# Normalization coefficients of a scan kernel: part of their arithmetic moved to GpSimd and TensorE, with the stages of five groups set further apart

## The chip, the cores and the metric

One core of a Trainium2 chip runs one program. The engines are TensorE (PE, matmuls; its weight loads are shown as PEld), VectorE (DVE), ScalarE (ACT), GpSimd (POOL) and SyncE (SP, which here only issues DMAs). Each has a queue of its own that it works through in order, and semaphores tie them together. The metric is the device time of the program in microseconds (us), as the median of several executions; lower is better.

## The reference

Two layers of the same form work on x of shape (32, 48, 64, 128): batch, channels, rows, columns, in float32. A layer normalizes its input over groups of three channels, then runs four recurrences over it, and adds the result to its input:

```python
def _gn(v, G=16, eps=1e-5):
    g = v.reshape(B_, G, C_ // G, H_, W_)
    m = jnp.mean(g, axis=(2, 3, 4), keepdims=True)
    s = jnp.var(g, axis=(2, 3, 4), keepdims=True)
    return ((g - m) / jnp.sqrt(s + eps)).reshape(v.shape)
def step(w, b):
    def f(carry, inp):
        nxt = inp + _conv1d(carry, w, b)
        return (nxt, nxt)
    return f
...
x = x + _L0_conv_ref(_gn(x), ...)
x = x + _L1_conv_ref(_gn(x), ...)
```

Within a layer the recurrence goes down the rows, up again, then right along the columns, and left again. Each step is a convolution of five taps (48 to 48 channels) over the other image axis, applied to the state of the step before. So a layer has 63 + 63 steps over rows and 127 + 127 over columns that depend on each other.

What the change touches is `_gn`: the mean and the variance of each image and channel group have to become a scale and an offset for each channel (scale = 1/sqrt(var + eps), offset = −mean × scale).

## The kernel before, in words

**Tiling.** The 32 images are worked on in four groups of eight (GB = 8). Eight neighbouring positions times 48 channels fill three tiles of 128 partitions (NG = 3). A step (`step`, L693) is nine matmuls of 128x128 (L706), 128 columns wide, into three PSUM tiles; each PSUM tile is evicted by one DVE operation (L715) that adds the bias and the step's input and writes the new state. The next step's matmuls read it.

**Phases.** `PHASES` (L102) lists twelve phases: for each layer four row phases (one for each group of images, 126 steps) and two column phases (one for each pair of groups, 254 steps). Together they are 2,024 steps, run one after the other.

**The agenda.** All other work is put between the steps by hand. `at(t, fn, ...)` (L785) books a function for step t of the whole scan; `catch_up` (L1124) calls what is due ahead of each step, and `in_order` (L231) fixes the order of the instructions on each engine to the order of these calls. `spread(t, gen, 1)` (L788) calls a generator once at each step from t on: each `yield` in it pushes what follows one step later. So an instruction stands in its engine's queue behind all that was booked earlier, and if it waits, everything behind it in that queue waits too: on PE and DVE that is the scan.

**The coefficients.** `scaling` (L289) makes scale and offset of one group of eight images. It first takes the means and variances of parts from one of three classes: `InputStats` (for the input, groups x0 to x3), `ResultStatsV` (for layer 0's result, statistics by DVE) and `ResultStatsA` (the same, with sums taken by ACT); for the result the groups are r0 to r3. The classes' `__call__` merges the parts. Then `average` sums over the three channels of a group by matmuls with a mask (L298), `expand` brings the result back to all partitions by three matmuls (L302), and short DVE operations stand between: differences from the mean (L325), their squares (L326), the variances added (L327), and at the end a reciprocal (L348) of ACT's Sqrt (L344), one Newton step (L350 to L353), scale (L360) and offset (L361). A float32 matmul of these shows as two passes on PE in the trace. For the input there is one mask (n = 1), and `average` and `expand` of the mean are done with the same source; for the result there are three (n = 3), and the average is copied out of PSUM before it is expanded.

**When.** x0 is done ahead of the scan, in `first_group`. x1, x2 and x3 are booked in `plan_input` (L798, L816): x1 ends in phase 0, x2 runs in phase 2 (the first column phase) around step 410, x3 in phase 4. r0 and r1 run in phase 3 around steps 557 and 577, r2 and r3 in phase 7, twenty steps apart (L932, L933).

**What runs beside them.** GpSimd adds the residuals of a column phase (`add_residual`, L635, L638), six units of 128x2048 for each quarter of the columns; it also permutes pieces of the input (`permute`, L536, sixteen copies of 112x256 for each piece of four rows for both halves), fills weight tiles with zeros (L266) and keeps a row (booked at L841, shown as L236). ACT applies the coefficients (`scale_rows`, L579, 24 or 48 operations for a load) and takes statistics of the input (`take_others`, L395 and L403) and of the result (L470, L476). In phase 3 group 3 of the input is brought in through one buffer: each piece's permutes and statistics must be through before the next piece's load can write there.

Of the kernel before, what the change touches and what calls it, by code (L numbers as in the profile page):

```python
# [31 lines left out]
ALU = mybir.AluOpType  # L32
# [9 lines left out]
GB = 8  # L42
# [76 lines left out]
def kernel(  # L119
# [166 lines left out]
    def stat_tile(shape, name, key):  # L286
        return stat_pool.tile(shape, F32, tag=name, name=f"{name}_{key}")

    def scaling(key, layer, g, averages, masks):  # L289
# [3 lines left out]
        yield from averages(key)  # L293
        mean_p, var_p = averages.result

        def average(ps, rhs):
            for i in range(n):
                nc.tensor.matmul(ps, masks[i], rhs[:, i], start=i == 0, stop=i == n - 1)  # L298

        def expand(ps, rhs):  # L300
            for o in range(NG):
                nc.tensor.matmul(ps[:, o], maskp[:, o], rhs, start=True, stop=True)  # L302
# [9 lines left out]
        mean_c = stat_tile([P, GB], "mean_c", key)  # L312
        nc.vector.tensor_copy(mean_c, ps[0:P, 0])
        yield
        if n > 1:
            expand(ps[:, 1 : 1 + NG], mean_c)
            yield
        mean = small("mean")
        if n > 1:
            nc.vector.tensor_copy(mean, ps[:, 1 : 1 + NG])  # L320
        at = mean if n > 1 else mean_c.unsqueeze(1)
        np_ = FULL if n > 1 else P
        spare = small("dev")
        dev = spare[0:np_, 0:n]
        nc.vector.tensor_tensor(dev, mean_p, at, ALU.subtract)  # L325
        nc.vector.tensor_tensor(dev, dev, dev, ALU.mult)  # L326
        nc.vector.tensor_tensor(dev, dev, var_p, ALU.add)  # L327
        yield
        if n == 1:
            expand(ps[:, 2 + NG :], dev[:, 0])  # L330
            nc.vector.tensor_copy(mean, ps[:, 1 : 1 + NG])
        else:
            average(ps[0:P, 1 + NG], dev)
# [12 lines left out]
        yield  # L346
        r0 = std
        nc.vector.reciprocal(r0, std)  # L348
        t0 = spare
        nc.vector.tensor_tensor(t0, var, r0, ALU.mult)  # L350
        nc.vector.tensor_tensor(t0, t0, r0, ALU.mult)
        yield
        nc.vector.tensor_scalar(t0, t0, -0.5, 1.5, ALU.mult, ALU.add)  # L353
# [6 lines left out]
        nc.vector.tensor_tensor(scale, r0, t0, ALU.mult)  # L360
        nc.vector.scalar_tensor_tensor(offset, mean, -1.0, scale, ALU.mult, ALU.mult)  # L361
        coeffs[layer, g] = scale, offset

    class InputStats:
# [48 lines left out]
        def __call__(self, key):  # L413
            mv = self.mv
            yield
# [772 lines left out]
```

## Time and profile before

| | us |
|---|---|
| three runs, median (lowest to highest) | 4323.13 (4319.51 to 4324.4) |
| the profiled execution, its time | 4327.19 |
| its span in the trace | 4325.4 |
| PE busy in the span | 4072.9 |
| DVE busy | 2177.4 |
| ACT busy | 1337.2 |
| GpSimd busy | 891.9 |

The scan itself lasts from the end of step 0 at 113.6 us to the end of the last step at 4241.5 us; the last results then go out until the end of the span. The mean granted clock of PE was 0.979 of full speed. The 6,072 evictions by DVE last 348 ns each; they are the beat by which steps are counted in what follows, step 0 being the first of phase 0.

A word on reading: in the timeline a row gives the start, the length, the engine, the source line, the operation, what it writes and reads, the shape, how many instructions the row merges, and in brackets the engine's idle time ahead of the first one with what ended it. A view by groups has the busy time and the mean of one in place of start and length.

The groups of DVE operations that belong to the coefficients, each four times over the program unless noted (mean of one):

| line | for x (112x8 or 128x24) | for r (128x24) |
|---|---|---|
| L313 copy of the mean from PSUM | 158 ns | 155 ns |
| L325 difference | 1100 ns | 183 ns (two groups of two) |
| L326 square | 1323 ns | 184 ns |
| L327 variance added | 1322 ns | 182 ns (two groups of two) |
| L348 reciprocal | 296 ns | 295 ns |
| L350, L351 Newton step | 252, 355 ns | 183, 182 ns |
| L353 Newton step, L360 scale | 280, 365 ns | 168, 183 ns |
| L361 offset | 274 ns | 183 ns |

### The profile page before, as it was taken

Reading aid. Unit: us, or ns where it says so; the run is one execution under the profiler, and the core shown is the slowest. Engines: PE = TensorE matmul, PEld = TensorE weight load, DVE = VectorE, ACT = ScalarE, POOL = GpSimd, SP = SyncE. Lnnn points to the kernel's source line nnn. Section 1 sums busy time; section 2 is a strip of 40 time slices with the busy share of each in tenths; the row PEclk is TensorE's granted clock in tenths of the full one; section 3 lists DMA queues with packets and bytes.
Section 4 is the critical chain, followed back from the end, with each engine's and each line's share of the span. In section 5 each row is a group of like instructions: output and inputs, shape, how many; then the busy total and the mean of one; then the engine's idle time right before and its main releaser. Section 6 shows DMA issues by size and latency. Waiting matters only on the chain. (4 is left out here: it accounts for less than half of the span.)

```text
span 4325.4 us, 89999 instructions
## 1 busy us (share of the span) xinstructions
PE 4072.9 (94%) x36624; PEld 4042.5 (93%) x36624; DVE 2177.4 (50%) x6554; ACT 1337.2 (31%) x2656; POOL 891.9 (21%) x859
## 2 busy tenths in 40 slices
PE   3898998998999999998999999999999999999992
PEld 1898998998999999998999999999999999999992
DVE  6344444446764445444446655444444444444443
ACT  1683301344794554300005773513000002110122
POOL 3472001234323010000004310000000024510352
PEclk9999999999999999999999999999999999999996
DMA  9999799966998989769507989929289049999999
GB/s 165 183 188 166 111 157 158 235 130 191 237 204 138 158 152 159 117 115 174 131 1 218 220 173 144 153 45 160 47 136 202 1 77 242 249 241 158 176 197 183
DMA packets 2117983, 680.35 MB, mean 157 GB/s; under 512 B 2006688, under 2 KB 2057408, under 8 KB 2077632
## 3 DMA queue, kind: packets, MB, share of 16 engines
q1 hardware_dynamic: 2019552, 582.30, 71.9%
q10 hardware_dynamic: 94816, 86.00, 9.7%
q0 software_dynamic: 3200, 6.30, 0.6%
q8 instruction: 288, 4.72, 0.5%
q14 instruction: 127, 1.04, 0.1%
HBM read 397.57 MB, written 295.99 MB: 160 GB/s over the span
## 5 line engine op out<-in xcount | busy, mean ns | idle before, releaser
L579 ACT ACTIVATE arena<-arena,offset,scale 128x256 f32<-128x256 f32 (+2 forms) x816 | 576.4, 800 | 423.9 <-PE step_12u L706 120.5
L638 POOL TENSOR_TENSOR arena<-arena 128x2048 f32<-128x2048 f32 x80 | 362.8, 4548 | 1469.2 <-PE step_10l L706 459.0
L536 POOL COPY arena<-arena 112x256 f32<-112x256 f32 x458 | 271.2, 651 | 561.5 <-DMA arena<-in_x 282.6
L706 PE MATMUL step_00r<-arena,early 128*128 128x128 f32 x2286 | 252.4, 274 | 15.3 <-DMA arena<-upa 14.2
L706 PEld LDWEIGHTS step_00r<-arena,early 128*128 128x128 f32 x2286 | 251.9, 187 | 15.8 <-issue 15.8
L706 PE MATMUL step_01r<-arena,early 128*128 128x128 f32 x2286 | 251.6, 274 | 14.0 <-DMA arena<-upa 14.0
L706 PEld LDWEIGHTS step_01r<-arena,early 128*128 128x128 f32 x2286 | 251.4, 187 | 14.2 <-issue 14.1
L706 PE MATMUL step_11r<-arena,early 128*128 128x128 f32 x2286 | 252.1, 274 | 8.6 <-DVE arena L715 8.6
L706 PEld LDWEIGHTS step_11r<-arena,early 128*128 128x128 f32 x2286 | 251.6, 187 | 9.0 <-DVE arena L715 8.9
L470 ACT ACTIVATE early<-arena 128x256 f32<-128x256 f32 x192 | 129.6, 675 | 412.2 <-DMA arena<-xin 319.9
L706 PE MATMUL step_00l<-arena,wleft 128*128 128x128 f32 x2286 | 252.2, 274 | 0.0
L706 PEld LDWEIGHTS step_00l<-arena,wleft 128*128 128x128 f32 x2286 | 251.8, 187 | 0.0
L706 PE MATMUL step_10l<-arena,wleft 128*128 128x128 f32 x2286 | 249.1, 272 | 0.0
L706 PE MATMUL step_11l<-arena,wleft 128*128 128x128 f32 x2286 | 249.1, 272 | 0.0
L706 PE MATMUL step_01l<-arena,wleft 128*128 128x128 f32 x2286 | 249.1, 272 | 0.0
L706 PE MATMUL step_10r<-arena,early 128*128 128x128 f32 x2286 | 249.1, 272 | 0.0
L706 PEld LDWEIGHTS step_10l<-arena,wleft 128*128 128x128 f32 x2286 | 249.0, 186 | 0.0
L706 PEld LDWEIGHTS step_11l<-arena,wleft 128*128 128x128 f32 x2286 | 249.0, 186 | 0.0
L706 PEld LDWEIGHTS step_01l<-arena,wleft 128*128 128x128 f32 x2286 | 249.0, 186 | 0.0
L706 PEld LDWEIGHTS step_10r<-arena,early 128*128 128x128 f32 x2286 | 249.0, 186 | 0.0
L663 ACT COPY arena<-arena 128x256 f32<-128x256 f32 x172 | 99.6, 656 | 404.2 <-POOL arena L638 152.9
L403 ACT ACTIVATE early<-arena 112x512 f32<-112x512 f32 x192 | 121.1, 631 | 305.6 <-DMA arena<-in_x 237.7
(176 smaller groups left out, 7070.1 us busy)
## 6 DMA issues: line engine op xcount, KB each, us to landing
arena<-in_x SPq DMA_DIRECT2D x48, 768.0 KB, 12.7
xin<-arena SPq DMA_DIRECT2D x96, 384.0 KB, 5.6
arena<-xin SPq DMA_DIRECT2D x96, 384.0 KB, 8.9
mid<-arena SPq DMA_DIRECT2D x96, 384.0 KB, 7.9
arena<-mid SPq DMA_DIRECT2D x192, 192.0 KB, 4.3
upb<-arena SPq DMA_DIRECT2D x192, 192.0 KB, 3.9
arena<-upb SPq DMA_DIRECT2D x96, 384.0 KB, 12.7
arena<-xin SPq DMA_DIRECT2D x186, 192.0 KB, 4.2
```

Source lines behind the costliest of these rows:

```text
L403: nc.scalar.activation(junk[0:P], piece, AF.Identity, accum_out=self.sum[:, at[0], at[1]],)
L470: nc.scalar.activation(junk[:, 0:n], view[:, b], AF.Identity, accum_out=self.sum[:, i, j : j + 1])
L536: copy(dst[:, r, q], src[:, r0 + r, q])
L579: nc.scalar.activation(args[0], args[0], AF.Identity, bias=args[2], scale=args[1])
L638: eng.tensor_tensor(unit, unit, nat, ALU.add)
L663: copy(by_w(perm)[:, a], src[:, a])
L706: nc.tensor.matmul(part(whole(ps[o])[0:m], -s), weights[:, i, at : at + m], part(src(i), s), start=seen[o] == 1, stop=seen[o] == left[o],)
```

## The change

Four things are changed in `scaling` and in the classes ahead of it.

- The difference from the mean reads the mean in PSUM, where `expand` or `average` left it. With one mask the copy of the mean into SBUF goes, and with it one step of distance.
- The variances are no longer added to the squares by DVE: `average` (three masks) and `expand` (one mask) take two terms and add them in PSUM, so such a group of matmuls doubles.
- With `slack` above 0, the squares, the Newton step, scale and offset, and in the classes' `__call__` the differences, squares and sums of the parts, are issued on GpSimd instead of DVE. Operations that multiply and add in one (`scalar_tensor_tensor`) are split in two, on either engine. The reciprocal, the reductions and all that reads PSUM stay on DVE.
- With `slack`, that many more steps lie ahead of the matmuls that read the squares, ahead of the reciprocal, and (in the classes) ahead of the reduction of the variances. `slack` is 8 for x2 and for r0 to r3, and 0 for x0, x1 and x3.

In the changed kernel's program SP's queue has the same 2,522 instructions in the same order. GpSimd has 47 instructions more, DVE 46 fewer, PE 24 matmuls more; ACT has the same ones, with some Sqrts at another place.

```diff
--- before.py
+++ after.py
@@ -286,20 +286,31 @@
     def stat_tile(shape, name, key):
         return stat_pool.tile(shape, F32, tag=name, name=f"{name}_{key}")
 
-    def scaling(key, layer, g, averages, masks):
+    def scaling(key, layer, g, averages, masks, slack=0):
 
 
         n = len(masks)
-        yield from averages(key)
+        yield from averages(key, slack)
         mean_p, var_p = averages.result
-
-        def average(ps, rhs):
-            for i in range(n):
-                nc.tensor.matmul(ps, masks[i], rhs[:, i], start=i == 0, stop=i == n - 1)
-
-        def expand(ps, rhs):
+        pool = nc.gpsimd if slack else nc.vector
+
+        def average(ps, *terms):
+            for k, rhs in enumerate(terms):
+                for i in range(n):
+                    nc.tensor.matmul(
+                        ps,
+                        masks[i],
+                        rhs[:, i],
+                        start=k == 0 and i == 0,
+                        stop=k == len(terms) - 1 and i == n - 1,
+                    )
+
+        def expand(ps, *terms):
             for o in range(NG):
-                nc.tensor.matmul(ps[:, o], maskp[:, o], rhs, start=True, stop=True)
+                for k, rhs in enumerate(terms):
+                    nc.tensor.matmul(
+                        ps[:, o], maskp[:, o], rhs, start=k == 0, stop=k == len(terms) - 1
+                    )
 
         def small(name):
             return stat_tile([FULL, NG, GB], name, key)
@@ -309,28 +320,27 @@
         if n == 1:
             expand(ps[:, 1 : 1 + NG], mean_p[:, 0])
         yield
-        mean_c = stat_tile([P, GB], "mean_c", key)
-        nc.vector.tensor_copy(mean_c, ps[0:P, 0])
-        yield
+        mean = small("mean")
+        spare = small("dev")
+        dev = spare[0 : FULL if n > 1 else P, 0:n]
         if n > 1:
+            mean_c = stat_tile([P, GB], "mean_c", key)
+            nc.vector.tensor_copy(mean_c, ps[0:P, 0])
+            yield
             expand(ps[:, 1 : 1 + NG], mean_c)
             yield
-        mean = small("mean")
-        if n > 1:
-            nc.vector.tensor_copy(mean, ps[:, 1 : 1 + NG])
-        at = mean if n > 1 else mean_c.unsqueeze(1)
-        np_ = FULL if n > 1 else P
-        spare = small("dev")
-        dev = spare[0:np_, 0:n]
-        nc.vector.tensor_tensor(dev, mean_p, at, ALU.subtract)
-        nc.vector.tensor_tensor(dev, dev, dev, ALU.mult)
-        nc.vector.tensor_tensor(dev, dev, var_p, ALU.add)
+            nc.vector.tensor_tensor(dev, mean_p, ps[:, 1 : 1 + NG], ALU.subtract)
+        else:
+            nc.vector.tensor_tensor(dev, mean_p, ps[0:P, 0:1], ALU.subtract)
+        nc.vector.tensor_copy(mean, ps[:, 1 : 1 + NG])
+        pool.tensor_tensor(dev, dev, dev, ALU.mult)
         yield
+        for _ in range(slack):
+            yield
         if n == 1:
-            expand(ps[:, 2 + NG :], dev[:, 0])
-            nc.vector.tensor_copy(mean, ps[:, 1 : 1 + NG])
+            expand(ps[:, 2 + NG :], dev[:, 0], var_p[:, 0])
         else:
-            average(ps[0:P, 1 + NG], dev)
+            average(ps[0:P, 1 + NG], dev, var_p)
             yield
             var_c = stat_tile([P, GB], "var_c", key)
             nc.vector.tensor_copy(var_c, ps[0:P, 1 + NG])
@@ -344,21 +354,24 @@
         nc.scalar.activation(std, var, AF.Sqrt)
         yield
         yield
+        for _ in range(slack):
+            yield
         r0 = std
         nc.vector.reciprocal(r0, std)
         t0 = spare
-        nc.vector.tensor_tensor(t0, var, r0, ALU.mult)
-        nc.vector.tensor_tensor(t0, t0, r0, ALU.mult)
+        pool.tensor_tensor(t0, var, r0, ALU.mult)
+        pool.tensor_tensor(t0, t0, r0, ALU.mult)
         yield
-        nc.vector.tensor_scalar(t0, t0, -0.5, 1.5, ALU.mult, ALU.add)
+        pool.tensor_scalar(t0, t0, -0.5, 1.5, ALU.mult, ALU.add)
         scale, offset = (
             stat_pool.tile(
                 [FULL, NG, GB], F32, tag=f"{t}{layer}{g}", name=f"{t}{layer}{g}"
             )
             for t in ("scale", "offset")
         )
-        nc.vector.tensor_tensor(scale, r0, t0, ALU.mult)
-        nc.vector.scalar_tensor_tensor(offset, mean, -1.0, scale, ALU.mult, ALU.mult)
+        pool.tensor_tensor(scale, r0, t0, ALU.mult)
+        pool.tensor_tensor(offset, mean, scale, ALU.mult)
+        pool.tensor_scalar(offset, offset, -1.0, None, ALU.mult)
         coeffs[layer, g] = scale, offset
 
     class InputStats:
@@ -410,8 +423,9 @@
                     at = slice(i, i + k)
                     nc.scalar.mul(self.neg[:, :, at], self.sum[:, :, at], -1.0 / BN)
 
-        def __call__(self, key):
+        def __call__(self, key, slack):
             mv = self.mv
+            pool = nc.gpsimd if slack else nc.vector
             yield
             if self.nv < GB:
                 n = GB - self.nv
@@ -421,14 +435,15 @@
                 nc.vector.tensor_copy(mv[:, 0, self.nv :, 0], mean)
                 yield
                 dev = self.neg
-                nc.vector.tensor_tensor(
+                pool.tensor_tensor(
                     dev, dev, mean.unsqueeze(2).to_broadcast([P, n, NBN]), ALU.add
                 )
-                nc.vector.tensor_tensor(dev, dev, dev, ALU.mult)
+                pool.tensor_tensor(dev, dev, dev, ALU.mult)
                 yield
-                nc.vector.scalar_tensor_tensor(
-                    dev, self.dev2, 1.0 / BN, dev, ALU.mult, ALU.add
-                )
+                pool.tensor_scalar(self.dev2, self.dev2, 1.0 / BN, None, ALU.mult)
+                pool.tensor_tensor(dev, dev, self.dev2, ALU.add)
+                for _ in range(slack):
+                    yield
                 var = stat_tile([P, GB], "var_x", key)[:, 0:n]
                 nc.vector.tensor_reduce(var, dev, mybir.AxisListType.X, ALU.add)
                 nc.vector.tensor_scalar(mv[:, 0, self.nv :, 1], var, 1.0 / NBN, None, ALU.mult)
@@ -445,7 +460,7 @@
             view = nat.rearrange("p (n b) -> p b n", b=GB)
             nc.vector.bn_stats(self.st[:, g * GB + b, 6 * j : 6 * (j + 1)], view[:, b])
 
-        def __call__(self, key):
+        def __call__(self, key, slack):
             mv = stat_tile([FULL, NG, GB, 2], "mv_r", key)
             for g in range(NG):
                 for b in range(GB):
@@ -481,21 +496,23 @@
                     accum_out=self.dev2[:, i, j : j + 1],
                 )
 
-        def __call__(self, key):
+        def __call__(self, key, slack):
             n = UNIT // GB
+            pool = nc.gpsimd if slack else nc.vector
             mean = stat_tile([FULL, NG * GB], "mean_r", key)
             nc.vector.tensor_reduce(mean, self.sum, mybir.AxisListType.X, ALU.add)
             nc.vector.tensor_scalar(mean, mean, 1.0 / (NQ * n), None, ALU.mult)
             yield
             dev = self.neg
-            nc.vector.tensor_tensor(
+            pool.tensor_tensor(
                 dev, dev, mean.unsqueeze(2).to_broadcast([FULL, NG * GB, NQ]), ALU.add
             )
-            nc.vector.tensor_tensor(dev, dev, dev, ALU.mult)
+            pool.tensor_tensor(dev, dev, dev, ALU.mult)
             yield
-            nc.vector.scalar_tensor_tensor(
-                dev, self.dev2, 1.0 / n, dev, ALU.mult, ALU.add
-            )
+            pool.tensor_scalar(self.dev2, self.dev2, 1.0 / n, None, ALU.mult)
+            pool.tensor_tensor(dev, dev, self.dev2, ALU.add)
+            for _ in range(slack):
+                yield
             var = stat_tile([FULL, NG * GB], "var_r", key)
             nc.vector.tensor_reduce(var, dev, mybir.AxisListType.X, ALU.add)
             nc.vector.tensor_scalar(var, var, 1.0 / NQ, None, ALU.mult)
@@ -813,7 +830,7 @@
             if j + ahead < len(times):
                 free = t + 7
                 at(free, take_in, g, 2 * rows * (j + ahead), nat)
-        spread(t + work + lag + (0, 2, 32, 5)[g], scaling(f"x{g}", 0, g, stats, x_masks), 1)
+        spread(t + work + lag + (0, 2, 32, 5)[g], scaling(f"x{g}", 0, g, stats, x_masks, (0, 0, 8, 0)[g]), 1)
 
     def plan_rows(k, t0, prev):
         if k == 1:
@@ -929,8 +946,8 @@
         if layer == 0:
             t = units[-1][0] + 14
             g = 2 * pair
-            spread(t, scaling(f"r{g}", 1, g, stats[0], r_masks), 1)
-            spread(t + 20, scaling(f"r{g + 1}", 1, g + 1, stats[1], r_masks), 1)
+            spread(t, scaling(f"r{g}", 1, g, stats[0], r_masks, 8), 1)
+            spread(t + 20, scaling(f"r{g + 1}", 1, g + 1, stats[1], r_masks, 8), 1)
         if layer:
 
             at(left + 10, nc.scalar.copy, junk[:, BN - 1 :], quarter(k, 3)[:, 0, 0, RUN - 1 : RUN])
```

## The prediction

> **What bounds the kernel now.** I read the page first. PE is busy in nearly every slice, ACT and GpSimd (POOL) are mostly free, and DVE is busy half the time.
>
> ```profile
> PE   3898998998999999998999999999999999999992
> DVE  6344444446764445444446655444444444444443
> POOL 3472001234323010000004310000000024510352
> ```
>
> Each digit is a share of 108 us in tenths. The kernel is one serial scan of 2,024 steps, nine matmuls and three DVE evictions (L715) each, and a step waits for the one before it. So an auxiliary instruction costs only what it adds to a step. I therefore went to the timeline of DVE and measured the distance between the third evictions of neighbouring steps: 1.98 us in a row phase, 1.96 in a column phase, in some 96 of 100 steps. All that is above this adds to 143 us over the scan. Around the statistics of layer 1's image group 2 (r2), undisturbed, it reads:
>
> ```profile
> 2586.31 0.54 DVE L715 SCALAR_TENSOR_TENSOR arena<-step_11d,bd,arena 128x128 f32<-128x128 f32 x2
> 2587.00 0.35 DVE L715 SCALAR_TENSOR_TENSOR arena<-step_11d,bd,arena 128x128 f32<-128x128 f32 x1
> 2587.26 1.11 DVE L452 BATCH_NORM_AGGREGATE mv_r_r<-bn_r 128x2 f32<-128x24 f32 x8
> 2588.29 0.54 DVE L715 SCALAR_TENSOR_TENSOR arena<-step_11d,bd,arena 128x128 f32<-128x128 f32 x2
> 2588.98 0.35 DVE L715 SCALAR_TENSOR_TENSOR arena<-step_11d,bd,arena 128x128 f32<-128x128 f32 x1 [0.15 <-PE step_11d L706]
> ...
> 2591.56 0.35 DVE L715 SCALAR_TENSOR_TENSOR arena<-step_11d,bd,arena 128x128 f32<-128x128 f32 x1 [0.28 <-PE step_11d L706]
> ...
> 2593.54 0.35 DVE L715 SCALAR_TENSOR_TENSOR arena<-step_11d,bd,arena 128x128 f32<-128x128 f32 x1 [0.28 <-PE step_11d L706]
> ...
> 2596.19 0.35 DVE L715 SCALAR_TENSOR_TENSOR arena<-step_11d,bd,arena 128x128 f32<-128x128 f32 x1 [0.28 <-PE step_11d L706]
> ```
>
> 1.11 us of DVE work costs the scan nothing (2587.00 to 2588.98 is 1.98). But the steps to 2591.56 and 2596.19 are 2.58 and 2.65: each holds six PE passes of an average (+0.60) or of an expansion (+0.67). PE has no room; DVE has about 1 us a step. So moving short DVE work off DVE is worth nothing where nothing disturbs it, and matmuls are never free.
>
> Two coefficient groups do stop the scan. Group x2 (third group of the input), in the DVE timeline, with GpSimd's beside it:
>
> ```profile
> 986.56 0.35 DVE L715 SCALAR_TENSOR_TENSOR arena<-step_00l,bd,arena 128x128 f32<-128x128 f32 x1 [0.28 <-PE step_00l L706]
> ...
> 991.63 3.61 DVE L325 TENSOR_TENSOR dev_x<-mv_x_x,mean_c_x 112x8 f32<-112x8 f32 x1
> 995.28 4.42 DVE L326 TENSOR_TENSOR dev_x<-dev_x 112x8 f32<-112x8 f32 x1
> 999.73 4.42 DVE L327 TENSOR_TENSOR dev_x<-dev_x,mv_x_x 112x8 f32<-112x8 f32 x1
> ...
> 1009.65 0.35 DVE L715 SCALAR_TENSOR_TENSOR arena<-step_00l,bd,arena 128x128 f32<-128x128 f32 x1 [0.93 <-PE step_00l L706]
> ```
> ```profile
> 986.22 26.86 POOL L638 TENSOR_TENSOR arena<-arena 128x2048 f32<-128x2048 f32 x6 [32.27 <-PE step_00l L706]
> ```
>
> Operations of eight elements, 154 to 166 ns elsewhere, last as long as one of GpSimd's additions (4.5 us). Four steps take 23.1 us instead of 7.8, with 0.6 in the fifth: 15.9 lost.
>
> Group r1 stops it otherwise:
>
> ```profile
> 1361.86 0.35 DVE L715 SCALAR_TENSOR_TENSOR arena<-step_02u,bd,arena 128x128 f32<-128x128 f32 x1 [0.29 <-PE step_02u L706]
> 1372.07 0.30 DVE L348 RECIPROCAL std_r<-std_r 128x24 f32<-128x24 f32 x1 [9.85 <-ACT std_r L344]
> ```
>
> The reciprocal is two steps behind the Sqrt in DVE's queue, but the Sqrt stands on ACT behind statistics of input group 3, whose third piece landed only at 1358.9. That costs 9.4 us and 1.6 in the step after, where PE runs slower: 11.0.
>
> [...]4.42 us beside additions of 4.55, while evictions (PSUM and SBUF) keep 0.35. [...]here the granted clock of 1361 to 1376 is 0.66, and a stop of D costs about D + 1.2.
>
> **The change part by part.** Prices on GpSimd: no small two-input operation is in the trace. 4548/2048 is 2.2 ns an element, and the copy of 112x16 elements is 198 ns, so I estimate 0.25 us for 24 elements and 0.4 for 96. Bounds: 0.2 and 1 each.
>
> *x2: −13.7.* The difference now reads PSUM, so it has one SBUF input. The square goes to GpSimd and the variance is added by PE. The square stands behind two additions of residuals and then waits for the difference at about 1005 (987 + 8 steps + 2); it doesn't queue. The expansion reads it eight steps later, 16 us of cover. What stays: average and expansion of the mean 0.88, expansion with two terms, twelve passes, 1.34. 15.9 − 2.2 = 13.7. Additions three to six fall behind the square, some 10 us later, but the next that needs them is 1064. The Sqrt gets behind two units of ACT statistics (13.7 us each, about 1014 to 1028); the reciprocal, ten steps after the Sqrt, comes at 1043. Bounds: −12 and −15.
>
> *r0 and r1: −1.0.* Here GpSimd's order bites. The order of the instructions in the changed kernel puts r0's square behind the first eight copies (L536) of group 3's second piece, and r1's four statistics operations behind the first eight of its third:
>
> ```profile
> 1324.92 9.49 POOL L536 COPY arena<-arena 112x256 f32<-112x256 f32 x16 [22.11 <-DMA taps<-in_w]
> 1358.93 9.40 POOL L536 COPY arena<-arena 112x256 f32<-112x256 f32 x16 [24.07 <-DMA arena<-in_x]
> ```
>
> r0's second average, at 1308.4 on PE, moves eight steps to 1324.2. Its square can't be there before 1324.9 + 4.7 + 0.25 = 1329.9. PE, with the whole scan behind that matmul, waits 5.7; with the slower clock +6.9. r1's reduction of the variance, DVE, comes ten steps after L487's 1335.8: 1355.6 + 6.9 + 0.6 = 1363.1; GpSimd is through at 1358.9 + 4.7 + 4 × 0.35 = 1365.0: DVE waits, and the evictions behind it, +1.9. The 11.0 of the Sqrt goes: it now has ten steps and the third piece is long done (fourth piece's ACT work ends at 1409.3, reciprocal at about 1420). Averages with two terms: 2 × 0.6 = +1.2. Sum −11.0 + 6.9 + 1.9 + 1.2 = −1.0. Bounds: −10 if the copies come in time, +12 if the piece lands as late as the fourth did.
>
> *r2 and r3: +1.2.* GpSimd is idle from 2541 to 2608, so no wait; two averages with six more passes each. The DVE work that they lose was covered by the 1 us.
>
> *x3: +0.9.* Same place, all on DVE: expansion +0.67, two more small operations, mostly covered, +0.2.
>
> *x1: +0.8.* As x3, but beside GpSimd copies (DVE operations of 0.5 us there): +0.67 and up to 1; half of it vanishes in the 16.5 us wait for ACT's scaling at step 141. Bounds 0 and 2.
>
> *x0: 0.* Before the scan. It gains 0.8 on DVE, loses 1.3 on PE and about 0.9 on the split offset: +1.4. ACT's scaling then waits for loads at 137 to 144 and the scan for it (12.0 us at step 15), which hides it; without this cover +1.4.
>
> Sum: −13.7 − 1.0 + 1.2 + 0.9 + 0.8 = −11.8. The profiled execution took 4327.19 us (span 4325.4), so 4315.4; it lies 4.1 over the median of 4323.13, on which I put the forecast: 4311.3. No queue of DMAs has a new order; SP's is the same list. The gain at x2 passes on if what follows is tied to the scan: GpSimd's additions at 1064.9, 1188.3 and 1238.6 are released by PE, so yes.
>
> **Rivals.** *Absorbed* (0.23): group 3's pieces don't move with the scan, so the 13.7 is waited for at r0 and r1. For it: SP issues without a pause from about 1160 to 1283. Against it: PE releases the additions before them. −11.8 + 12.5: about 4324.
> *No wait at GpSimd* (0.11): the second piece lands some 6 us earlier relative to the scan. −11.8 − 8.8: about 4302.
> *Slower* (0.13): GpSimd's queue stops the scan. One mechanism, one place: r0's square behind the second piece. That piece took 13.3 us to load (from ACT's last read of the one buffer, 1311.5, to 1324.8), the fourth 24.6 (1371.8 to 1396.4). If the second takes 24.6 as well and isn't tied to the scan, r0 waits 5.7 + 11.3 + 12: −11.8 + 11.3 + 12.5 = +12, 4335. It decides from where the piece lands 12 us later relative to the scan than now. Against it: nothing in the change adds a DMA.
>
> **How the numbers follow.** Forecast 0.53 at 4311, its own range 4305 to 4318 from the bounds. 0.2% is 8.6 us, about what a measurement here can tell from none. Faster by more: 0.48 of the forecast and the second rival, 0.59. Same: 0.05 and most of the first, 0.27. Slower: 0.14. The range for eight in ten runs from the second rival to just past the first: 4302 to 4325.
>
> **What would show it.** The steps at x2 at 2.84 and 3.3 us and no DVE operation over 1 us there; PE waiting for GpSimd's dev_r at r0, about 6 us, and DVE under 3 at r1; no wait of the reciprocal for ACT; r2 and r3 with one average at +1.2. It is wrong if the scan waits for a GpSimd operation in x2, or if a step before 1300 gives the 13.7 back.

## The result, and the profile after

| | before | after |
|---|---|---|
| median of six runs each, us (lowest to highest) | 4324.7 (4319.51 to 4328.77) | 4311.74 (4302.9 to 4313.56) |
| profiled span, us | 4325.4 | 4309.7 |

The ratio is 0.9966, with a 95% interval of 0.9956 to 0.9976: 0.3% faster. The first two parts of the page of the kernel after (each digit of a row again a share in tenths):

```profile
span 4309.7 us, 90123 instructions
PE 4080.8 (95%) x36672; PEld 4051.4 (94%) x36672; DVE 2161.1 (50%) x6508; ACT 1337.0 (31%) x2656; POOL 904.1 (21%) x906
...
PE   4898998999999999998999999999999999999992
...
DVE  6344444446654454444446654444444444444443
...
POOL 4571011325322020000005310000000024420352
```

No engine's busy time tells of the gain: PE has 7.9 us more than before, DVE 16.3 less. What counts are the stops. From here on "loss" is what a stretch of steps takes above the beat of 1.98 us (1.96 in column phases), measured as in the prediction between the third evictions of neighbouring steps. Evictions are L732 here, PE's matmuls of the steps L723, GpSimd's additions L655, its copies of the input L553.

**x2.** DVE's timeline, the place where three operations took 12.5 us before:

```profile
997.48 0.35 DVE L732 SCALAR_TENSOR_TENSOR arena<-step_00l,bd,arena 128x128 f32<-128x128 f32 x1 [0.28 <-PE step_00l L723]
997.75 0.15 DVE L334 TENSOR_TENSOR dev_x<-mv_x_x,ps_x 112x8 f32<-112x8 f32 x1
997.81 0.18 DVE L335 COPY mean_x<-ps_x 128x24 f32<-128x24 f32 x1
...
998.54 0.61 DVE L732 SCALAR_TENSOR_TENSOR arena<-step_00l,bd,arena 128x128 f32<-128x128 f32 x2
999.44 0.35 DVE L732 SCALAR_TENSOR_TENSOR arena<-step_00l,bd,arena 128x128 f32<-128x128 f32 x1 [0.28 <-PE step_00l L723]
```

GpSimd's timeline beside it:

```profile
983.05 4.53 POOL L655 TENSOR_TENSOR arena<-arena 128x2048 f32<-128x2048 f32 x1
997.98 0.20 POOL L336 TENSOR_TENSOR dev_x<-dev_x 112x8 f32<-112x8 f32 x1 [10.39 <-DMA arena<-xin]
998.16 18.08 POOL L655 TENSOR_TENSOR arena<-arena 128x2048 f32<-128x2048 f32 x4
```

The step that holds the difference takes its 1.96 us (997.48 to 999.44). The square follows on GpSimd as soon as the difference is there (the bracket names a DMA, but DVE's difference ended only 0.08 us before), and the other four additions come behind it. Steps 406 to 445 lose 2.26 us instead of 16.03. GpSimd had finished two additions at 987.58 (the second is shown) and then stood 10.39 us with nothing running, because the square, in its queue ahead of the other additions, wasn't ready. So no addition ran beside the difference, and this trace doesn't show whether reading the mean from PSUM was needed; e5 below tries that alone.

**r0.** GpSimd, PE and DVE where r0's second average stands (start, length, and in brackets the idle time with what ended it):

```profile
1306.10 4.70 POOL L553 COPY arena<-arena 112x256 f32<-112x256 f32 x8 [20.55 <-DMA taps<-in_w]
1310.77 0.22 POOL L336 TENSOR_TENSOR dev_r<-dev_r 128x24 f32<-128x24 f32 x1
1310.94 4.67 POOL L553 COPY arena<-arena 112x256 f32<-112x256 f32 x8
```
```profile
1299.74 7.53 PE L723 MATMUL step_02u<-arena,early 128*96 128x120 f32 x67
1311.04 1.29 PE L300 MATMUL ps_r<-dev_r,mask_in 128*112 128x8 f32 x6 [3.77 <-POOL dev_r L336]
1312.18 1.27 PE L300 MATMUL ps_r<-mv_r_r,mask_in 128*112 128x8 f32 x6
```
```profile
1307.31 0.35 DVE L732 SCALAR_TENSOR_TENSOR arena<-step_02u,bd,arena 128x128 f32<-128x128 f32 x1 [0.28 <-PE step_02u L723]
1315.78 0.78 DVE L732 SCALAR_TENSOR_TENSOR arena<-step_02u,bd,arena 128x128 f32<-128x128 f32 x2 [8.12 <-PE step_02u L723]
1317.48 0.35 DVE L732 SCALAR_TENSOR_TENSOR arena<-step_02u,bd,arena 128x128 f32<-128x128 f32 x1 [0.93 <-PE step_02u L723]
```

An operation of 0.22 us stands behind eight copies that wait for the piece's load (it landed at 1305.86; the bracket names a load of weights that landed just after it), PE waits for it 3.77 us, and one step takes 10.17 us (1307.31 to 1317.48). The wait costs nearly twice its length (8.2 us over the beat, 7.0 of them without the added passes), because PE comes back at a granted clock of 0.50:

```profile
1290.00:1307.00 17.00, 17.00 (x157) 17.00 (x156) 8.30 (x27) 4.06 (x11) 0.90 (x2) 1.00 0.64 97
1307.00:1311.00 4.00, 0.27 (x3) 0.08 (x1) 0.38 (x2) 3.84 (x11) 4.00 (x9) 0.98 0.27 48
1311.00:1314.00 3.00, 2.96 (x15) 2.96 (x16) 0.00 (x0) 2.84 (x10) 3.00 (x6) 0.50 0.16 24
1314.00:1318.00 4.00, 4.00 (x23) 4.00 (x22) 1.12 (x4) 3.87 (x10) 2.06 (x4) 0.54 0.17 24
```

These are windows of the same trace: bounds, length, busy time of PE, PE's weight loads, DVE, ACT and GpSimd, then the granted clock (1.00, 0.98, 0.50, 0.54), DMA share and GB/s.

**r1.** Its four operations on GpSimd stand behind the third piece's copies; DVE reads their result:

```profile
1344.63 0.39 POOL L513 TENSOR_TENSOR neg_r<-neg_r,dev_r 128x96 f32<-128x96 f32 x1
```
```profile
1346.30 0.24 DVE L517 TENSOR_REDUCE var_r_r<-neg_r 128x24 f32<-128x96 f32 x1
```

They are through at 1345.02, the reduction comes at 1346.30 and waits for nothing. The reciprocal (L360) waits for no Sqrt either: the old stop of 11.0 us is gone. All of r0 and r1 (steps 557 to 620) loses 13.49 us, before 16.13.

**x3** lost more than before: 6.50 us in steps 715 to 735, before 2.38. DVE's timeline, then GpSimd's:

```profile
1610.82 0.21 DVE L433 TENSOR_REDUCE mean_x_x<-sum_x_x 112x8 f32<-112x64 f32 x1
1611.06 2.96 DVE L434 TENSOR_SCALAR mean_x_x<-mean_x_x 112x8 f32<-112x8 f32 x1
...
1614.14 0.86 DVE L732 SCALAR_TENSOR_TENSOR arena<-step_10u,bd,arena 128x128 f32<-128x128 f32 x3
1617.57 0.22 DVE L438 TENSOR_TENSOR neg_x_x<-neg_x_x,mean_x_x 112x64 f32<-112x64 f32 x1 [2.57 <-ACT early L408]
```
```profile
1604.55 9.45 POOL L553 COPY arena<-arena 112x256 f32<-112x256 f32 x16 [16.94 <-DMA arena<-in_x]
```

L434, which the change doesn't touch, takes 2.96 us and ends with the last of the sixteen copies (1614.00); then DVE, with evictions behind it, waits 2.57 us for ACT's statistics of the same piece. The same place before, DVE and GpSimd:

```profile
1630.79 0.21 DVE L419 TENSOR_REDUCE mean_x_x<-sum_x_x 112x8 f32<-112x64 f32 x1
1631.03 0.17 DVE L420 TENSOR_SCALAR mean_x_x<-mean_x_x 112x8 f32<-112x8 f32 x1
```
```profile
1621.11 9.50 POOL L536 COPY arena<-arena 112x256 f32<-112x256 f32 x16 [16.20 <-DMA arena<-in_x]
```

There the reduction came 9.7 us after the copies began and just after they ended; now 6.3 us after. The scan had come forward by 20.0 us here, the copies by 16.6.

### The profile page after: what moved, and what is told of

Same layout as the page of the kernel before. It is cut to its first block, busy times and chain, and to the rows that moved or that the text cites. A ratio compares the mean times of both kernels' runs of the same rounds, so it can differ in the third digit from the quotient of the medians.

```text
span 4309.7 us, 90123 instructions
## 1 busy us (share of the span) xinstructions
PE 4080.8 (95%) x36672; PEld 4051.4 (94%) x36672; DVE 2161.1 (50%) x6508; ACT 1337.0 (31%) x2656; POOL 904.1 (21%) x906
## 5 line engine op out<-in xcount | busy, mean ns | idle before, releaser
L596 ACT ACTIVATE arena<-arena,offset,scale 128x256 f32<-128x256 f32 (+2 forms) x816 | 576.0, 799 | 399.2 <-DMA arena<-xin 154.7
L655 POOL TENSOR_TENSOR arena<-arena 128x2048 f32<-128x2048 f32 x80 | 362.9, 4550 | 1384.8 <-PE step_10l L723 473.2
L553 POOL COPY arena<-arena 112x256 f32<-112x256 f32 x458 | 271.0, 649 | 535.3 <-DMA arena<-in_x 404.6
L723 PE MATMUL step_01r<-arena,early 128*128 128x128 f32 x2286 | 251.6, 274 | 16.0 <-DMA arena<-upa 16.0
L723 PEld LDWEIGHTS step_01r<-arena,early 128*128 128x128 f32 x2286 | 251.4, 187 | 16.3 <-issue 16.2
L723 PE MATMUL step_00r<-arena,early 128*128 128x128 f32 x2286 | 251.3, 273 | 16.2 <-DMA arena<-upa 16.2
L723 PEld LDWEIGHTS step_00r<-arena,early 128*128 128x128 f32 x2286 | 251.0, 187 | 16.6 <-issue 16.6
L723 PE MATMUL step_11r<-arena,early 128*128 128x128 f32 x2286 | 252.6, 274 | 5.5 <-DVE arena L732 5.5
L723 PEld LDWEIGHTS step_11r<-arena,early 128*128 128x128 f32 x2286 | 252.1, 187 | 5.9 <-DVE arena L732 5.8
L723 PE MATMUL step_00l<-arena,wleft 128*128 128x128 f32 x2286 | 249.6, 272 | 0.0
L723 PE MATMUL step_10r<-arena,early 128*128 128x128 f32 x2286 | 249.3, 272 | 0.0
L723 PEld LDWEIGHTS step_10r<-arena,early 128*128 128x128 f32 x2286 | 249.1, 186 | 0.2 <-DVE arena L732 0.2
L723 PEld LDWEIGHTS step_00l<-arena,wleft 128*128 128x128 f32 x2286 | 249.2, 186 | 0.0
L723 PE MATMUL step_10l<-arena,wleft 128*128 128x128 f32 x2286 | 249.1, 272 | 0.0
L723 PE MATMUL step_11l<-arena,wleft 128*128 128x128 f32 x2286 | 249.1, 272 | 0.0
L723 PE MATMUL step_01l<-arena,wleft 128*128 128x128 f32 x2286 | 249.1, 272 | 0.0
L723 PEld LDWEIGHTS step_10l<-arena,wleft 128*128 128x128 f32 x2286 | 249.0, 186 | 0.0
L723 PEld LDWEIGHTS step_11l<-arena,wleft 128*128 128x128 f32 x2286 | 249.0, 186 | 0.0
L723 PEld LDWEIGHTS step_01l<-arena,wleft 128*128 128x128 f32 x2286 | 249.0, 186 | 0.0
## 6 DMA issues: line engine op xcount, KB each, us to landing
arena<-upb SPq DMA_DIRECT2D x96, 384.0 KB, 11.8
```

The costliest lines, as they stand in the source:

```text
L553: copy(dst[:, r, q], src[:, r0 + r, q])
L596: nc.scalar.activation(args[0], args[0], AF.Identity, bias=args[2], scale=args[1])
L655: eng.tensor_tensor(unit, unit, nat, ALU.add)
L723: nc.tensor.matmul(part(whole(ps[o])[0:m], -s), weights[:, i, at : at + m], part(src(i), s), start=seen[o] == 1, stop=seen[o] == left[o],)
```

## The experiments

Every kernel was profiled once and timed together with the kernel before; kernels timed together share those runs. The median of the kernel before was 4324.7 us beside the result, 4319.2 beside the repeat and e1 to e3, 4319.8 beside e4, e5, e6 and e8, and 4318.3 beside e9, so the ratios can be compared and the absolute times only roughly. Intervals are 95%. The losses below are each of one profiled execution.

| kernel | median (lowest to highest, runs) | ratio to before | end of the scan in the trace |
|---|---|---|---|
| the changed kernel again | 4310.71 (4299.68 to 4322.03, 20) | 0.9979 [0.9972, 0.9987] | 4226.5 |
| e1_x2_only | 4303.76 (4299.75 to 4309.02, 5) | 0.9970 [0.9957, 0.9983] | 4220.1 |
| e2_r_only | 4316.98 (4312.03 to 4325.34, 12) | 0.9997 [0.9988, 1.0005] | 4230.9 |
| e3_r_square_dve | 4308.65 (4302.49 to 4318.74, 20) | 0.9978 [0.9972, 0.9985] | 4218.5 |
| e5_psum_difference | 4319.61 (4316.28 to 4326.54, 10) | 1.0000 [0.9991, 1.0010] | 4241.0 |
| e6_x2_later | 4303.98 (4296.17 to 4309.41, 6) | 0.9965 [0.9953, 0.9978] | 4217.5 |
| e8_r0_earlier | 4307.96 (4303.81 to 4324.87, 10) | 0.9975 [0.9965, 0.9984] | 4241.2 |
| e4_two_shifts | 4306.62 (4298.51 to 4312.55, 7) | 0.9969 [0.9957, 0.9980] | 4217.8 |
| e9_x3_later | 4307.43 (4291.43 to 4315.59, 11) | 0.9971 [0.9959, 0.9983] | 4217.6 |

**1. The change, repeated and taken apart.** The first run is the changed kernel as it is.

> The changed kernel once more, for the spread of what the change doesn't touch. My theory: the step costs at the coefficients come back within 0.3 us (x2: 0.88 and 1.34; r0: about 8.2; doubled averages 1.19), as they are set by the order of the queues; the start of the scan, the first steps of the column phases and the late stop in the last phase, where before and after differed by -4.8, +2.0, +2.0 and -3.1 us, move by some us either way. Time 4306 to 4314. Rival: these differences belong to the change, and come back the same within 0.5 us.

It gave x2 2.26 us, r0/r1 16.01, r2/r3 6.33, x3 5.85. The terms of x2 and r2/r3 repeat; x3 differs by 0.7 us and r0/r1 by 2.5, more than the 0.3 expected, since there the wait hangs on when a load lands (PE waited 5.70 us for r0's square in this one). Of the other stretches, the start came back as early as in the first trace (step 0 ends at 108.2 us, there at 107.8, before at 113.6), while the last phase (steps 1801 to 2023), 2.5 us shorter than before in the first trace, was 0.1 shorter in this one.

e1 has the new coefficients for x2 and the old ones elsewhere; e2 the new ones for r0 to r3 and the old ones for all x groups. The lines that choose them, shortened and read against the kernel before:

```diff
-spread(... scaling(f"x{g}", 0, g, stats, x_masks), 1)
+spread(... (scaling(..., 8) if g == 2 else scaling_old(...)), 1)     # e1
+spread(t, scaling(f"r{g}", 1, g, stats[0], r_masks, 8), 1)           # e2
+spread(t + 20, scaling(f"r{g + 1}", 1, g + 1, stats[1], r_masks, 8), 1)
```

> Only group x2 has the new coefficients with slack 8; all other groups have the old ones. Theory (two-input DVE operations beside GpSimd's additions): the stop of 15.9 us at x2 goes, 13.7 us of it net, some 4 of these come back in phase 3 where ACT's scaling waits for loads; r0 has no stop, r1 keeps its 9 to 11 us for the Sqrt. Time 4311 to 4315, as fast as the whole change. Rival (the gain comes from the Sqrt's distance in the r groups or from fewer DVE operations everywhere): x2 alone gives under 4 us, 4321 or more.

> The new coefficients with slack 8 only in r0 to r3; the x groups are the old ones. Theory (order of GpSimd's queue): r1's stop of 11 us goes, r0 stops for 6 to 8 us at its average behind copies of group 3's second piece, four doubled averages cost 2.4; x2 keeps its 15.9 us. Sum -11 + 7 + 2.4 = about -2: 4322 to 4325. Rival: the r groups are free of waits, -11 + 2.4: 4316 or less.

x2 alone loses the same 2.26 us at x2 and is 0.3% faster; the r groups alone can't be told from no change. In e2 steps 557 to 620 lose 11.80 us and steps 1189 to 1250 6.35. So the gain of the whole is x2's; e1 gained somewhat more than expected, and the 4 us that were to come back in phase 3 didn't. The medians don't add up: −15.4 and −2.2 us against the kernel before in the same measurement, but −8.5 with both and the new x0, x1 and x3. The intervals allow about 7 us of doubt on that gap of 9; the loss at x3 (part 5 below) can be some 4 us of it, but differs between executions, and the rest stays open.

**2. Is it DVE's work that x2 saved, or a coincidence?** e6 is the kernel before with one number changed; nothing is moved off DVE:

```diff
-spread(t + work + lag + (0, 2, 32, 5)[g], scaling(f"x{g}", 0, g, stats, x_masks), 1)
+spread(t + work + lag + (0, 2, 50, 5)[g], scaling(f"x{g}", 0, g, stats, x_masks), 1)
```

> The kernel before, with one number changed: x2 starts 18 steps later, so that its operations stand where GpSimd has finished its six additions. Nothing moves to GpSimd and no matmul is added. Theory: the wait is only a matter of what GpSimd does at that moment; the three operations take 0.15 to 0.2 us, x2 costs 1.6 us (its two groups of six passes) instead of 15.9, so 14 us below before and as fast as the whole change. Rival (DVE's work itself is what costs, so it has to leave DVE): x2 keeps 10 us or more. Risk: the reciprocal, two steps after the Sqrt, waits for ACT's statistics; then a new stop of up to 13 us.

The same three operations, eighteen steps later, in DVE's timeline:

```profile
1020.33 0.16 DVE L325 TENSOR_TENSOR dev_x<-mv_x_x,mean_c_x 112x8 f32<-112x8 f32 x1
1020.52 0.17 DVE L326 TENSOR_TENSOR dev_x<-dev_x 112x8 f32<-112x8 f32 x1
1020.72 0.17 DVE L327 TENSOR_TENSOR dev_x<-dev_x,mv_x_x 112x8 f32<-112x8 f32 x1
```

GpSimd around it:

```profile
984.14 22.61 POOL L638 TENSOR_TENSOR arena<-arena 128x2048 f32<-128x2048 f32 x5
1043.94 4.53 POOL L638 TENSOR_TENSOR arena<-arena 128x2048 f32<-128x2048 f32 x1 [37.19 <-PE step_00l L706]
```

Between 1006.75 and 1043.94 GpSimd adds nothing, and x2 loses 1.68 us, less than in the changed kernel (no doubled expansion). The wait of the reciprocal for ACT, named as a risk, doesn't come. The stop was the meeting with GpSimd's additions; the arithmetic on DVE was never the cost.

e5 is the kernel before with only the difference reading PSUM:

```diff
+        at = ps[:, 1 : 1 + NG] if n > 1 else ps[0:P, 0:1]
         nc.vector.tensor_tensor(dev, mean_p, at, ALU.subtract)
```

> The kernel before, with one edit: the difference from the mean reads the mean in PSUM (one SBUF input); squares and the added variances stay on DVE with two SBUF inputs. Theory (a DVE operation with two SBUF inputs waits for the GpSimd addition that runs): at x2 the difference falls from 3.6 to about 0.15 us, the square waits for the rest of the running addition (up to 4.5) and the third operation for a whole one (4.4); the stop at x2 falls from 15.9 to 10 to 13 us. Rival (any short DVE operation is slow beside GpSimd): the difference stays above 3 us. Time 2 to 5 us below before.

```profile
990.61 0.15 DVE L326 TENSOR_TENSOR dev_x<-mv_x_x,ps_x 112x8 f32<-112x8 f32 x1
990.79 3.41 DVE L327 TENSOR_TENSOR dev_x<-dev_x 112x8 f32<-112x8 f32 x1
994.24 4.42 DVE L328 TENSOR_TENSOR dev_x<-dev_x,mv_x_x 112x8 f32<-112x8 f32 x1
...
1008.15 4.01 DVE L351 TENSOR_TENSOR dev_x<-var_x,std_x 128x24 f32<-128x24 f32 x1
```
```profile
985.20 26.92 POOL L639 TENSOR_TENSOR arena<-arena 128x2048 f32<-128x2048 f32 x6 [36.19 <-PE step_00l L707]
```

The timelines of DVE and GpSimd in e5 (its lines stand one later than before): beside the additions, the operation with one input in PSUM takes 0.15 us (3.61 before), the two behind it with both inputs in SBUF take 3.41 and 4.42 us. They end at 994.20 and 998.66, where by estimate the second and third addition end (994.17 and 998.66, with six equal parts of the 26.92 us). So of three operations of the same size beside the same additions, the one with an input in PSUM wasn't held up and the two with both in SBUF were; one trace shows it, for these alone. And since the group now came on earlier, a Newton operation that had run after the additions fell beside the last of them (4.01 us). x2 lost 15.45 us, not the 10 to 13 expected, and the time didn't fall (ratio 1.0000, where 2 to 5 us were expected): a stop moved, not removed.

**3. The stop at r0, and what stands behind it.** e3 leaves the squares of the r groups on DVE; e8 starts r0 three steps earlier, so that its square is ahead of the copies in GpSimd's queue:

```diff
-        pool.tensor_tensor(dev, dev, dev, ALU.mult)                           # e3
+        (pool if n == 1 else nc.vector).tensor_tensor(dev, dev, dev, ALU.mult)
-            spread(t, scaling(f"r{g}", 1, g, stats[0], r_masks, 8), 1)        # e8
+            spread(t - (0 if pair else 3), scaling(f"r{g}", 1, g, stats[0], r_masks, 8), 1)
```

> The changed kernel, but the squares of the r groups (one 128x24 operation each) stay on DVE. Theory: r0's stop at the average with two terms, 7 us beside the 1.2 of the matmuls, is the wait for that one GpSimd operation behind eight copies; the step falls from about 10.2 to 3.2 us. r1's four statistics operations then meet the scan 7 us earlier, behind eight copies of the third piece, so up to 5 of the 7 us may come back as a wait of DVE at the reduction of r1's variance. Time 4305 to 4311. Rival: the stop is PE's own (matmuls with two terms and the first one after a switch of operands): it stays at 7 us or more.

> The changed kernel, with r0 begun three steps earlier, so that its square stands ahead of the copies of group 3's second piece in GpSimd's queue, not behind them. Theory (order of GpSimd's queue): the stop of 7 to 9 us at r0's average goes, as in the run with the square on DVE, though the square stays on GpSimd; r1's wait behind the third piece then shows as 7 to 9 us. In sum within 3 us of the changed kernel. Rival (GpSimd's operation is slow[...]): r0's stop stays.

In both, r0's average takes its 3.17 us with six passes more and waits for nothing. So r0's stop was the order of GpSimd's queue: neither the matmuls with two terms nor a slow operation on GpSimd. Yet steps 557 to 620 lose 15.49 and 16.25 us, no less than the changed kernel (13.49 and 16.01). GpSimd and DVE at r1 in e3:

```profile
1340.41 4.67 POOL L553 COPY arena<-arena 112x256 f32<-112x256 f32 x8 [22.80 <-DMA arena<-in_x]
```
```profile
1339.12 0.35 DVE L732 SCALAR_TENSOR_TENSOR arena<-step_02u,bd,arena 128x128 f32<-128x128 f32 x1 [0.28 <-PE step_02u L723]
1346.75 0.25 DVE L517 TENSOR_REDUCE var_r_r<-neg_r 128x24 f32<-128x96 f32 x1 [7.29 <-POOL neg_r L513]
```

DVE now stands 7.29 us at the reduction, for r1's operations behind the third piece. The reduction is ready 7 us sooner than in the changed kernel, the piece is not (its copies start at 1340.4, there at 1338.6). I had thought that at most 5 us would come back; steps 588 to 590 lost 9.8, of which 0.6 is the price of an average. So the stop at r0 hid one at r1. (In e8 DVE waited 8.42 us at the same reduction. Its profiled execution was 17 us longer than its median; x3 alone lost 10.1 us in it, see part 5.)

**4. The Sqrt's stop without moving work.** e4 is e6 with eight steps more between Sqrt and reciprocal for r1 and r3, all on DVE as before:

```diff
+        for _ in range(late):
+            yield
         r0 = std
         nc.vector.reciprocal(r0, std)
...
+            spread(t + 20, scaling(f"r{g + 1}", 1, g + 1, stats[1], r_masks, 8), 1)
```

> The kernel before with two shifts and no other edit: x2 begins 18 steps later, and in r1 and r3 the reciprocal stands eight steps further from the Sqrt. Theory: x2 costs 1.6 instead of 15.9; r1's Sqrt is done when the reciprocal comes, so its 11 us go; no matmul is added. 22 to 26 us below before, about 10 below the changed kernel. Rival: the time saved is waited for at the loads of group 3 and at the scaling in phase 3: not over 14 us below before.

Steps 557 to 620 lose 5.15 us, which is just the matmuls' price (r2 and r3, undisturbed, lost 5.14 before): the stop of the Sqrt is gone, and none at GpSimd has come in its place. But steps 663 to 665 then lost 7.9 us, where e6 and the changed kernel lose nothing. DVE's timeline there (L717 is the eviction in this kernel, L581 the scaling by ACT):

```profile
1490.28 0.35 DVE L717 SCALAR_TENSOR_TENSOR arena<-step_10d,bd,arena 128x128 f32<-128x128 f32 x1 [0.28 <-PE step_10d L708]
1495.31 0.35 DVE L717 SCALAR_TENSOR_TENSOR arena<-step_10d,bd,arena 128x128 f32<-128x128 f32 x1 [4.68 <-DMA arena<-mid]
1496.77 0.61 DVE L717 SCALAR_TENSOR_TENSOR arena<-step_10d,bd,arena 128x128 f32<-128x128 f32 x2 [1.12 <-ACT arena L581]
```

The scan was 8.3 us ahead of e6 and ran into a load of the middle result (mid) and its scaling, which had not come forward; at the end of step 666 it was where e6 was (1506.41 and 1506.85). In this execution the gain at r1 was absorbed, and the median fits: 13.2 us below the kernel before, as the rival said, not 22 to 26.

**5. x3.** The changed kernel with x3 four steps later:

```diff
-(0, 2, 32, 5)[g], scaling(f"x{g}", 0, g, stats, x_masks, (0, 0, 8, 0)[g])
+(0, 2, 32, 9)[g], scaling(f"x{g}", 0, g, stats, x_masks, (0, 0, 8, 0)[g])
```

> The changed kernel with the coefficients of x3 begun four steps (8 us) later and nothing else. My reading of the changed kernel's trace: x3's statistics came 3.4 us early relative to the last piece of group 3, so a reduction on DVE met the sixteen copies on GpSimd (2.96 us for an operation of 0.17) and then ACT's last statistics. If so, steps 715 to 745 lose about 2.3 us over the beat (0.9 for the expansion of the mean as before, 1.3 for the one with two terms), where the changed kernel lost 6.5 and 5.9 in two executions; the end of the scan comes about 4 us earlier unless a later load takes it back. Rival: the loss at x3 is the price of the added operations themselves; then steps 715 to 745 stay at 5 us or more. Time: 4307 by the first, 4311 by the second, beside 4311.7 for the changed kernel; the whole program's differences of several us between executions may hide it, so the steps decide.

```profile
1613.94 0.21 DVE L433 TENSOR_REDUCE mean_x_x<-sum_x_x 112x8 f32<-112x64 f32 x1
1614.19 0.17 DVE L434 TENSOR_SCALAR mean_x_x<-mean_x_x 112x8 f32<-112x8 f32 x1
```
```profile
1601.09 9.49 POOL L553 COPY arena<-arena 112x256 f32<-112x256 f32 x16 [15.72 <-DMA arena<-in_x]
```

With the reduction 12.9 us after the start of the copies, L434 takes 0.17 us again and the steps lose 2.30 us, as expected. The whole time doesn't decide here (ratio 0.9971, the repeat 0.9979), the steps do. Four steps (7.9 us) less would have left it, by estimate, 4.9 us after the start. The other traces agree. Where the reduction comes 6.0 (e8), 6.3 (the changed kernel), 6.9 (its repeat) and 8.7 us (e4, old coefficients) after the start of the copies, this operation takes 3.18, 2.96, 2.30 and 0.52 us and ends each time within 0.03 us of the last copy; the steps lose 10.1, 6.5, 5.9 and 3.3. Where it comes 9.7 us or more after it (the kernel before, e1, e2, e3, e5, e6, e9), it takes 0.17 or 0.18 us and they lose at most 2.4. e3 has the changed coefficients at their unshifted place and is among these, at 11.7 us and a loss of 2.30: there the distance came out long enough by itself. So x3's extra loss was its place relative to the last piece, not its added operations, and it is not the same in every execution.

**Which version is best?** e2 and e5 are no faster than the kernel before. Of the others none is told apart from the whole change by its interval. e6, one number in the kernel before, has 0.9965 [0.9953, 0.9978]; the whole change 0.9966 and 0.9979 in two measurements. No gain of the 47 instructions on GpSimd over this shift can be seen.

## Why the prediction came true, point by point

The forecast of 4311 us and its sign hold (4311.74). By its own terms, in us, from the first trace of each kernel:

| term | predicted | measured |
|---|---|---|
| x2 | −13.7 | −13.8 (16.03 to 2.26, in every run with it) |
| r0 and r1 | −1.0 | −2.6 (16.13 to 13.49); −1.4 over several traces, see below |
| r2 and r3 | +1.2 | +1.2 (5.14 to 6.33) |
| x3 | +0.9 | +4.1; +3.5 in the second trace; −0.1 and +7.7 in e3 and e8, where x3 is the same |
| x1, with the wait at step 141 | +0.8 | +0.3 (23.0 to 23.3) |
| sum | −11.8 | −10.8 |

- **x2: right, with its cause, the meeting with the additions.** The bare difference in PSUM wasn't enough (e5), and another time was (e6). The prediction counted on the difference reading PSUM and on the additions falling behind the square; in the changed kernel's trace the second alone had cleared GpSimd when the difference came. That one input in PSUM would spare the difference was my estimate: the trace before showed only evictions, which read PSUM too, at 0.35 us beside the additions. e5 then measured 0.15 us for the difference.
- **r0: right in kind and in sum, its parts less so.** The square stood behind eight copies as predicted. The stop was to cost 6.9, as a wait of 5.7 and 1.2 for the slower clock; it cost 7.0 (10.17 − 1.98, less 1.2 for the added passes), but with a wait of 3.8 and 3.2 for the clock. That the two errors met is luck: in the repeat, e9 and e2 the same wait was 5.70, 5.19 and 3.40 us, and it cost 9.7, 9.3 and 5.3. The mis-sized part is the clock's 1.2, read from r1's stop before, after which PE was slow for some 3 us (a clock of 0.50 from 1372 to 1376, then 0.99 to 1380); here it was slow for some 6.6 (an estimate: 0.54 from 1314 to 1318 puts the end near 1317.7). What sets that length isn't shown.
- **r1: the stop of the Sqrt went, as predicted; the +1.9 at the variance reduction was 0.** The step that failed is the sum's assumption that the third piece keeps its distance to the scan: "1355.6 + 6.9 + 0.6 = 1363.1; GpSimd is through at ... 1365.0" was 1346.3 and 1345.0. So the operations were through 1.3 us before they were needed. As a mechanism it was right: e2 shows this wait at 1.17 us, and e3 at 7.29 once r0's stop no longer stood ahead. Traces with the new r groups (13.5, 16.0, 15.6 and 11.8) and with the old (16.1, 15.1, 17.8 and 13.3) average 14.2 and 15.6: −1.4, near the −1.0 predicted, with a spread larger than the difference.
- **x3: mis-sized.** The term was +0.9 for an expansion and two small operations. These are about right: e3 and e9 have 2.30 where traces with the old x3 that don't meet the copies have 1.59 to 2.38. What the term lacked was the place: a scan that comes forward meets loads that come forward less (here 20.0 and 16.6 us). The prediction weighs this for r0 and r1 and not for x3.
- **x1 and x0: absorbed, as predicted.** x1's own steps lose from 3.7 to 13.1 us in the traces, old code or new, and step 141 gives it back: the sum is 20.3 to 23.9 in all. The end of step 95, ahead of them, is at 321.7 us on average in six traces with the old x0 and at 320.8 in five with the new, between 316.6 and 326.4.
- **That the total fits to a microsecond is partly luck.** The errors at r0 and r1 (−1.6) and at x3 (+3.2) partly cancel. The measured difference was −13.0 us in the result and −8.5 in the repeat. And other stretches vary by several us between executions: the end of step 0 came 5.8 us earlier in the changed kernel's trace (it lies between 108.6 and 113.6 us in the traces with the old x0 and between 106.4 and 113.3 with the new, so it is not shown that x0 has a part in it), and steps 553 and 554 lost 4.4 more, waiting for a scaling by ACT (L596).
- **The rivals.** "Absorbed" didn't happen to x2's gain: r0 and r1 lost less than before, not 12.5 more, and e1 keeps it to the end. The mechanism exists, though, and it is what took e4's gain at r1 and four microseconds at x3. "No wait at GpSimd" needed the second piece to land 6 us earlier relative to the scan, which no trace shows. e3 and e8 took away r0's wait alone, and the gain didn't come, because r1's wait grew in its place. "Slower" needed a load of 24.6 us in front of r0's square; PE waited 3.4 to 5.7 us in four traces.

## What to carry to other kernels

Where short operations last as long as a neighbour's long one (here 4.42 us beside additions of 4.55), ask first whether they can run at another time: here a shift of eighteen steps gave what the move to another engine gave. An operation moved to an in-order queue inherits every wait ahead of it there (r0's square of 0.22 us made PE wait 3.77), so look for what the queue waits for at that moment, and for the next such place that the first stop hides. When a stop of D us is removed, follow the next few loads that the scan meets: what doesn't come forward with it takes the gain back, at once (e4, 7.9 us) or as a collision elsewhere (x3, some 4 us).

## What the runs showed of the hardware

- A DVE operation with a single SBUF input of eight elements (L434, TENSOR_SCALAR) stood 2.96 us beside copies on GpSimd that follow each other (sixteen in 9.45 us), until the last of them ended. In e9 it takes 0.17 us. The reduction just ahead of it (L433), also with one SBUF input, took 0.21 us in the midst of the same copies, as it does without them. So having one SBUF input doesn't settle it; what told the two apart no trace shows.
- Small operations on GpSimd in the changed kernel take 0.20 to 0.28 us for 8 or 24 elements a partition and 0.35 to 0.45 us for 96, against 0.17 to 0.18 us on DVE for 24; the estimates of 0.25 and 0.4 held.
- In the changed kernel a wait of PE of 3.77 us was followed by some 6.6 us at a clock of 0.50 (by the estimate above), which cost 3.2 us more. In three other traces (e2, e9, the repeat) waits of 3.40, 5.19 and 5.70 us cost 1.9, 4.1 and 4.0 us more.
